# A four-layer graph attention stack: layer 2's all-node rows moved to blocks 3, 7 and 6, two projections per half step at its end, and ten of layer 3's units at the border

## The chip, the cores and the metric

The kernel runs on one core of a Trainium2 chip. The metric is the device time of one execution in microseconds (us), lower is better. A profile is one execution recorded by the hardware profiler; its engines are PE (matmuls), PEld (the weight loads beside them), DVE (vector), ACT (activation), POOL (GpSimd) and SP (which here only issues DMAs). SPq and POOLq are the queues on which SP and POOL issue DMAs.

## The reference, cut to what matters

4096 nodes with 256 features pass through four attention layers over one adjacency (1 in 256 entries set, and the diagonal). Layers 0 and 1 have four heads, layer 2 has two, layer 3 has one head with a positive and a negative softmax. Each layer ends in residual and layer norm, and the result is the input of the next.

```python
e = leaky_relu(s1[:, None, :] + s2[None, :, :], ALPHA)        # layer 2
e = where(adj[:, :, None] == 1, e, NEG)
h_prime = einsum('ijh,jhc->ihc', softmax(e, axis=1), W3h)
...
e = leaky_relu(Wh1 + Wh2.T, ALPHA)                            # layer 3
attention = softmax(where(mask, e, NEG_INF), axis=1)
negative_attention = -softmax(where(mask, -e, NEG_INF), axis=1)
new_h_prime = concatenate([attention @ x, negative_attention @ x], axis=1) @ fc_W
...
x = layernorm(x + layer(x))                                   # each of the four
```

## The kernel before, in words

The 4096 rows are 32 row tiles of 128 (`NT`), and eight blocks of four row tiles (`BT`, `NB`). A row tile attends in one of two ways.

A **packed** row tile uses 14 positions of 128 neighbours (`NP`): 13 gathers of neighbour rows from DRAM, issued by POOL as indirect DMAs (L636), and its own row tile, loaded by SP (L633). It works in two halves of seven positions (`RowTile.half`): ACT makes the weights position by position (L689 for layers 0 to 2; L666, L667 and L669 for layer 3), DVE masks them (L690; L668 and L670), PE multiplies them with the gathered rows (L701). The first six positions of every row hold only neighbours from row tiles 0 to 16 (`FRONT`, `MIX`, `NODES`), so a first half needs the projected rows 0 to 16 only, and a second half needs all 32.

A block in the **all-node** way takes four row tiles against all 32 node tiles with no gather (`Layer.whole_rows`). A unit of it is one node tile: a load of its rows (`vw`, L917) and, every eighth unit, of a mask (`mw`, L915), ACT and DVE for the weights (L929 and L930 in layer 2; L932, L934 or L936, and L937 in layer 3), four accumulations on PE (L940). `WHOLE = (0, 0, 3, 1)` puts the last three blocks of layer 2 (row tiles 20 to 31) and the last one of layer 3 (28 to 31) in this way; a block of layer 2 is 32 units, the one of layer 3 is 64 (32 for each softmax). Their mask is stored to DRAM while the neighbour lists are made, in layer 0 (L392, 2112 KB a block).

A layer goes in half steps: `Layer.part(m, part)` loads the packed tiles m and m+1, and `half_with_whole` projects one finished row of the next layer, runs the packed half, then as many units as spread the all-node work evenly over the steps up to three tiles before the end (`whole`). A projection (`Projection`) is a transpose of the row (L538), its copy to SBUF by ACT (L543), eight matmul records (L552), the row's values by ACT and DVE (L570 to L578), their store (L580), a transpose of the score row (L584) and its store (L591).

At the border, `Layer.close` projects the open rows below `MIX`, loads the first half of the following layer's tile 0, finishes the last tile, runs that first half, projects the rest, loads the first halves of tiles 1 and 2, runs tile 1's, and loads tile 3's. What the instruction streams of the engines look like is decided by the scheduler of the tile framework, which interleaves them within the limits of the data and of the buffers; each engine then runs its stream in that order.

Gathered rows lie in two pools, `g0` with 16 buffers and `g1` with 14. A layer 3 position fills a buffer; before, first halves lie in `g0` and second halves in `g1`. The PSUM banks of projections come from one pool of two (`ptwo[1]` in layer 2).

Of the kernel before, what the change touches and what calls it, by code (L numbers as in the profile page):

```python
# [53 lines left out]
NT = N // P  # L54
KT = F // P
BT = 4
W = BT * P
NB = NT // BT
# [14 lines left out]
CAP = NG * P  # L73
HALF = NP // 2

GROUPS = (((24, 4),), ((28, 2),), ((16, 2), (20, 1), (31, 2)), ((28, 1), (31, 4)))
LEAD = 10
MIX = 17
FRONT = 6
# [15 lines left out]

WHOLE = (0, 0, 3, 1)

LEAST = 2.0611536224385579e-09  # L100

# [76 lines left out]
class Turns:  # L178


    def __init__(self, pools):
        self.pools = list(pools)
# [6 lines left out]
class Program:  # L189
# [98 lines left out]
    def lists(self, ctx):  # L288
# [55 lines left out]
        for j in range(NT):  # L344
            m = 0
# [18 lines left out]
        class Block:  # L364
# [23 lines left out]

            def places(self):
                blk = self.blk  # L390
                if blk >= NB - max(WHOLE):
                    nc.sync.dma_start(out=shared["maskW"][blk], in_=self.mk)  # L392
                hit = wk.tile([P, BT, NT], BF16, name="hit")
                nc.vector.tensor_scalar(hit, self.red, 0.0, None, op0=ALU.is_gt)
                flat = hit.rearrange("p t j -> p (t j)")
                nc.vector.memset(flat[:, blk * BT:blk * BT + (BT - 1) * (NT + 1) + 1:NT + 1], 0.0)
                pt = prog.bank(prog.pthree)
                nc.tensor.matmul(pt[:, :P], flat, ones, start=True, stop=True)
                totals = wk.tile([P, P], BF16, name="totals")
# [59 lines left out]
        prog = self  # L459
# [140 lines left out]
class RowTile:  # L600

    def __init__(self, layer, m):
        self.layer, self.m = layer, m
        self.slots = {}
        self.accs = None

    def place(self, pos):


        L, n = self.layer, self.layer.n
        per = 1 if n == 3 else 2
        s = pos // per
        if s not in self.slots:
            pool = L.prog.g1 if n > 0 and s * per >= HALF else L.prog.g0
            self.slots[s] = pool.tile([P, 2 * ROW[0]], F32, name="G")
        c = (pos % per) * ROW[n]
        return self.slots[s][:, c:c + ROW[n]]
# [20 lines left out]
    def half(self, half):  # L640
# [1 line left out]
        prog, sh, S = L.prog, L.shared, self.S  # L642
        H, Wd, V, T, A = HEADS[n], WIDTH[n], VALS[n], TERMS[n], LOGS[n]
        if self.accs is None:
            pool = prog.ptwo[1 if n == 3 and self.m % 2 else 0]
# [78 lines left out]
class Layer:  # L724
# [2 lines left out]

    def __init__(self, prog, n):
        self.prog, self.n, self.nc, self.shared = prog, n, prog.nc, prog.shared
        self.count = NT - WHOLE[n] * BT  # L730
        self.tiles = {}
        self.loaded = set()
        self.units = self.whole_rows()
        self.total = WHOLE[n] * NT * (1 if n < 3 else 2)
        self.used = 0
        self.nxt = self.middle = self.stored = self.between = None
        self.group = []
        self.ready = []
        self.step = 0
        self.last = ()  # L740


    def tile(self, m):
        if m not in self.tiles:
            self.tiles[m] = RowTile(self, m)
        return self.tiles[m]

    def load(self, m, half):
# [4 lines left out]
    def set_banks(self):  # L753
        self.prog.banks = self.prog.ptwo[1] if self.n in (0, 2) else self.prog.pthree

    def whole(self, step):

        while self.between is None and self.used < self.total \
                and self.used < self.total * (step + 1) / (2 * self.count - 6):
            next(self.units)  # L760
            self.used += 1
        if self.used == self.total:
            next(self.units, None)

# [15 lines left out]
    def half_alone(self, m, part):  # L780


        self.step = 2 * m + part
        proj, middle = None, self.middle
        second = m > NT - (LEAD if self.n == 0 else 6) and len(self.ready) > 1
        if self.ready and self.ready[0][0] < self.step and (part == 0 or second):
            self.set_banks()
            if part == 1 and self.n == 0:
                self.prog.banks = self.prog.pthree
            proj = Projection(self.prog, self.n + 1, self.nxt, *self.ready.pop(0)[1:])  # L790
            proj.transpose()
        if part == 1 or self.tile(m).accs is None:
            self.tile(m).half(part)
        if self.stored is not None:
            self.stored.store()
# [12 lines left out]
        if middle is not None:  # L808
            middle.edge()
        self.stored, self.middle = middle, proj  # L810

    def half_with_whole(self, m, part):

        proj = None
# [12 lines left out]
        if self.between is not None:  # L827

            self.last = self.between()
            self.between = None  # L830
        if self.stored is not None:
            self.stored.store()
            self.stored = None
        if proj is not None:
# [5 lines left out]
        if proj is not None:  # L840
            proj.row()
            proj.edge()
            self.stored = proj

    def steps(self):
        for m in range(self.count):
# [3 lines left out]
    def close(self, following):  # L850

        last = self.count - 1
        self.step += 2
        if self.stored is not None:
            self.stored.store()
        if self.middle is not None:
            self.middle.row()
            self.middle.edge()
# [3 lines left out]
            self.set_banks()  # L862
            Projection(self.prog, self.n + 1, self.nxt, *entry[1:]).all()
        if following is not None:
            following.load(0, 0)
        if WHOLE[self.n]:
            for _ in self.units:
                pass
            self.tile(last).finish()
            if following is not None:  # L870
                following.tile(0).half(0)
        else:
            self.set_banks()
            first = Projection(self.prog, self.n + 1, self.nxt, *self.ready.pop(0)[1:])
# [617 lines left out]
```

## Time and profile before

| | us |
|---|---|
| median of 3 executions | 2267.64 (2262.25 to 2268.71) |
| the profiled execution | 2271.01 |
| its span, first to last instruction | 2269.3 |
| busy PE, DVE, ACT, POOL | 2019.7, 1798.0, 1738.5, 1494.7 |
| layer 2's first matmul of a packed half | 1340.7 |
| layer 3's first and last gather | 1746.65, 2240.07 |

The profiled execution lies 1.7 us over its span and 3.4 us over the median. Busy times are sums over all four layers and hide that each stage has another limit; so the prediction reads the stage around the change.

### The profile page before, as it was taken

What the parts mean: (1) busy time and instruction counts of PE and PEld (TensorE: products, weight loads), DVE (VectorE), ACT (ScalarE), POOL (GpSimd) and SP (SyncE); (2) the same over time, 40 slices, a digit from 0 to 9 for tenths busy, and PEclk for the clock granted to TensorE, in tenths of its full rate; (3) what the DMA queues carried; (4) which work ended last, traced back from release to release, by engine and by line L of the source; (5) the groups of instructions that cost most, each with busy time, mean ns of one, the idle gap of its engine ahead of it and who ended that gap; (6) DMA issues with size and microseconds to landing.
All of it is one profiled execution on the core that took longest, in us unless ns stands there. A gap on an engine that the chain in (4) does not pass through costs nothing. (4 is left out here: it accounts for less than half of the span.)

```text
span 2269.3 us, 49072 instructions
## 1 busy us (share of the span) xinstructions
PE 2019.7 (89%) x15689; PEld 1834.6 (81%) x15689; DVE 1798.0 (79%) x5317; ACT 1738.5 (77%) x4977; POOL 1494.7 (66%) x1596
## 2 busy tenths in 40 slices
PE   3878889989999959998988897989998799999996
PEld 2757878887989949998878887989997688778885
DVE  2987999999999959988888886877975465576567
ACT  4777888988889949988888877978883666676664
POOL 2107565655667777777777777777761677777773
PEclk8988999999999979999999998999998899999998
DMA  8879767877557766666666666778764788888884
GB/s 281 264 229 356 237 213 248 292 240 233 143 163 194 211 165 167 190 177 174 166 173 176 172 169 180 216 206 239 221 200 138 236 268 269 274 266 276 266 256 145
DMA packets 250318, 492.98 MB, mean 217 GB/s; under 512 B 44385, under 2 KB 156610, under 8 KB 249666
## 3 DMA queue, kind: packets, MB, share of 16 engines
q0 software_dynamic: 81536, 245.30, 38.0%
q1 hardware_dynamic: 168514, 244.46, 33.7%
q8 instruction: 126, 2.06, 0.4%
q14 instruction: 142, 1.16, 0.2%
HBM read 437.05 MB, written 52.54 MB: 216 GB/s over the span
## 5 line engine op out<-in xcount | busy, mean ns | idle before, releaser
L636 POOL DMA_INDIRECT G<-vals,idx x1456 | 1481.7, 1018 | 736.4 <-issue 188.5
L689 ACT ACTIVATE w<-S,G 128x128 f32<-128x128 f32 x3248 | 988.2, 389 | 123.0 <-DMA G<-vals,idx 109.1
L698 PE MATMUL bank<-w,G 128*65 128x128 f32 x7168 | 843.8, 277 | 97.8 <-DVE w L686 75.7
L698 PEld LDWEIGHTS bank<-w,G 128*65 128x65 f32 x7168 | 796.4, 140 | 116.5 <-DVE w L686 86.9
L701 PE MATMUL bank<-G,w 128*128 128x257 f32 (+1 forms) x2688 | 491.1, 340 | 36.1 <-DVE w L690 12.5
L701 PEld LDWEIGHTS bank<-G,w 128*128 128x128 f32 x2688 | 431.8, 193 | 86.2 <-ACT z L1004 16.6
L690 DVE SCALAR_TENSOR_TENSOR w<-w,bank 128x896 f32<-128x896 f32 x384 | 410.6, 1079 | 18.7 <-ACT w L689 18.1
L940 PE MATMUL bank<-vw,pw 128*128 128x129 f32 (+1 forms) x2048 | 299.7, 303 | 5.6 <-ACT zw L1004 2.7
L940 PEld LDWEIGHTS bank<-vw,pw 128*128 128x128 f32 x2048 | 275.7, 193 | 22.4 <-ACT zw L1004 3.1
L666 ACT ACTIVATE w<-S,G 128x128 f32<-128x128 f32 x392 | 138.0, 390 | 130.0 <-DMA G<-vals 77.6
L435 DVE TENSOR_SCALAR oh<-iota,place 128x256 bf16<-128x256 f16 (+2 forms) x992 | 225.8, 301 | 9.3 <-PE bank L441 9.3
L441 PE MATMUL bank<-mk,oh 128*128 128x132 fp8e4 x2336 | 188.6, 226 | 12.4 <-DVE oh L435 10.2
L680 DVE TENSOR_TENSOR w<-S,G 128x256 f32<-128x256 f32 x384 | 154.0, 417 | 53.0 <-DMA G<-vals,idx 49.6
L552 PE MATMUL bank<-wext,xT 128*128 128x268 f32 (+3 forms) x640 | 181.4, 417 | 15.7 <-ACT xT L543 12.8
L441 PEld LDWEIGHTS <-oh 128*128 128x128 bf16 x2336 | 148.6, 99 | 48.3 <-DVE oh L435 20.4
L380 ACT ACTIVATE mk<-raw 128x1024 uint8<-128x1024 int32 x128 | 131.1, 1054 | 25.8 <-DMA raw<-in_adjB_dram 25.1
L552 PEld LDWEIGHTS bank<-wext,xT 128*128 128x128 f32 x640 | 119.2, 203 | 35.5 <-ACT xT L543 15.7
L929 ACT ACTIVATE pw<-Sw,d 128x512 f32<-128x512 f32 x192 | 131.7, 714 | 15.6 <-PE bank L940 11.9
L937 DVE TENSOR_TENSOR pw<-pw,mw 128x512 f32<-128x512 f32 x64 | 44.1, 693 | 125.0 <-ACT pw L936 61.6
L930 DVE SCALAR_TENSOR_TENSOR pw<-pw,mw 128x512 f32<-128x512 f32 x192 | 126.7, 690 | 17.3 <-ACT pw L929 16.4
L686 DVE SCALAR_TENSOR_TENSOR w<-w,bank 128x896 f32<-128x896 f32 x128 | 138.6, 1083 | 0.8
L690 DVE SCALAR_TENSOR_TENSOR w<-w,mk 128x896 f32<-128x896 f32 x80 | 86.7, 1087 | 47.5 <-ACT w L689 44.1
(131 smaller groups left out, 1605.3 us busy)
## 6 DMA issues: line engine op xcount, KB each, us to landing
raw<-in_adjB_dram SPq DMA_DIRECT2D x128, 512.0 KB
mk<-maskC SPq DMA_DIRECT2D x112, 231.0 KB
G<-vals,idx POOLq DMA_INDIRECT x1456
S<-edge SPq DMA_DIRECT2D x64, 256.0 KB
vw<-vals SPq DMA_DIRECT2D x96, 129.0 KB
xp<-y SPq DMA_DIRECT2D x96, 128.0 KB
y<-xp SPq DMA_DIRECT2D x96, 128.0 KB
mw<-maskW SPq DMA_DIRECT2D x20, 528.0 KB
```

The source lines that it names most:

```text
L435: nc.vector.tensor_scalar(oh[:, :n * P], iota[:, :n * P], self.place[:, it, j:j + 1], None, op0=ALU.is_equal)
L441: nc.tensor.matmul(accs[b][:, s * MC:(s + 1) * MC], oh[:, (k - a) * P:(k - a + 1) * P], mk[:, j, it, :].bitcast(FP8), start=touches[b][0] ...
L552: nc.tensor.matmul(pp[:, :c1 - c0], self.xT[:, k, :], wext[:, k, c0:c1], start=(k == 0), stop=(k == KT - 1 and brow is None))
L636: nc.gpsimd.indirect_dma_start(out=self.place(pos), out_offset=None, in_=sh["v"][n][:NODES[t], :], in_offset=bass.IndirectOffsetOnAxis(ap= ...
L666: nc.scalar.activation(w[0][:, k, :], S[:, 0, :], AF.Relu, bias=d(k, 0))
L680: nc.vector.tensor_tensor(w[h][:, k:k + 2, :], S[:, h:h + 1, :].to_broadcast([P, 2, P]), dd[:, :, V + T + h:V + T + h + 1].to_broadcast([P ...
L686: nc.vector.scalar_tensor_tensor(w[h], w[h], LEAST, mh, op0=ALU.max, op1=ALU.mult)
L689: nc.scalar.activation(w[h][:, k, :], S[:, h, :], AF.Exp, bias=d(k, h))
L690: nc.vector.scalar_tensor_tensor(w[h], w[h], LEAST, mh, op0=ALU.max, op1=ALU.mult)
L698: nc.tensor.matmul(accs[0][:Wd, h * P:(h + 1) * P], v, w[h][:, k, :], **how)
L701: nc.tensor.matmul(a, w[h][:, k, :], v, **how)
L940: nc.tensor.matmul(accs[it][:, c:c + Wd], p[:, it, :], v[:, c:c + Wd], start=(j == 0 and h == heads[0]), stop=(j == NT - 1), skip_group_ch ...
```

## The change

Layer 2's all-node blocks are given by number and in order: 3, 7, 6 (row tiles 12 to 15, 28 to 31, 24 to 27). Its packed tiles are then 0 to 11 and 16 to 23, in this order, again 20. Layer 3 keeps block 7. Rows ready for projection are taken with those below `MIX` first. In layer 2's last three tiles, once its units are used up, a half step takes two projections, the second with banks of the pool `pthree`. At the border to layer 3 the first halves of four tiles are loaded together; tile 0's first half is followed by six units of layer 3, and each of the two rows still open by two more (`AHEAD` = 10), and the remaining units are spread over the layer as before. Layer 3's buffers: first halves of tiles 0 and 1 in `g0`, of 2 and 3 in `g1`, the second halves of these four in `g0`, and from tile 4 on, whole tiles in `g1` (even) and `g0` (odd). Rows of layer 2 are normed in other groups (`GROUPS`). The mask of block 3 instead of block 5 is stored to DRAM.

```diff
-GROUPS = (((24, 4),), ((28, 2),), ((16, 2), (20, 1), (31, 2)), ((28, 1), (31, 4)))
+GROUPS = (((24, 4),), ((28, 2),), ((16, 2), (17, 1), (20, 2), (24, 1), (31, 2)), ((28, 1), (31, 4)))
-WHOLE = (0, 0, 3, 1)
+WHOLE = ((), (), (3, 7, 6), (7,))
+AHEAD = 10
+ORDER = tuple([m for m in range(NT) if m // BT not in w] for w in WHOLE)
...
-                if blk >= NB - max(WHOLE):
+                if any(blk in w for w in WHOLE):
                     nc.sync.dma_start(out=shared["maskW"][blk], in_=self.mk)
...
-            pool = L.prog.g1 if n > 0 and s * per >= HALF else L.prog.g0
+            if n == 3:
+                other = self.step % 2 == 0 if self.step > 3 else self.step > 1 and s < HALF
+            else:
+                other = n > 0 and s * per >= HALF
+            pool = L.prog.g1 if other else L.prog.g0
...
-                and self.used < self.total * (step + 1) / (2 * self.count - 6):
+                and self.used < self.ahead + (self.total - self.ahead) * (step + 1) / (2 * self.count - 6):
...
     def half_with_whole(self, m, part):
-        if self.ready and self.ready[0][0] < self.step:
-            _, y, row = self.ready.pop(0)
-            self.set_banks()
-            proj = Projection(self.prog, self.n + 1, self.nxt, y, row)
-            proj.transpose()
+        able = sorted((e for e in self.ready if e[0] < self.step), key=lambda e: e[2] >= MIX)
+        self.set_banks()
+        over = self.used == self.total and m > self.count - 4
+        for entry, banks in zip(able, (self.prog.banks, self.prog.pthree)[:1 + over]):
+            self.ready.remove(entry)
+            projs.append(Projection(self.prog, self.n + 1, self.nxt, *entry[1:], banks=(banks,) * 3))
+            projs[-1].transpose()
...
     def close(self, following):
-            following.load(0, 0)
+            for m in range(4 if following.n == 3 else 1):
+                following.load(m, 0)
...
                 following.tile(0).half(0)
+                following.ahead = AHEAD
+                for _ in range(AHEAD - 2 * len(self.ready)):
+                    following.unit()
...
         for _, y, m in self.ready:
             self.set_banks()
             Projection(self.prog, self.n + 1, self.nxt, y, m).all()
+            if WHOLE[self.n]:
+                following.unit()
+                following.unit()
...
-        for blk in range(NB - WHOLE[n], NB):
+        for blk in WHOLE[n]:
```

More of the change, by code (lines that the diff above doesn't have):

```diff
@@ L600, with __init__ @@
 class RowTile:
-    def __init__(self, layer, m):
-        self.layer, self.m = layer, m
+    def __init__(self, layer, step, m):
+        self.layer, self.step, self.m = layer, step, m
         self.slots = {}
@@ L644, in half @@
         if self.accs is None:
-            pool = prog.ptwo[1 if n == 3 and self.m % 2 else 0]
+            pool = prog.ptwo[1 if n == 3 and self.step % 2 else 0]
             self.accs = [prog.bank(pool) for _ in range(2 if n == 3 else 1)]
@@ L729, in __init__ @@
         self.prog, self.n, self.nc, self.shared = prog, n, prog.nc, prog.shared
-        self.count = NT - WHOLE[n] * BT
+        self.order = ORDER[n]
+        self.count = len(self.order)
         self.tiles = {}
@@ L733, in __init__ @@
         self.units = self.whole_rows()
-        self.total = WHOLE[n] * NT * (1 if n < 3 else 2)
-        self.used = 0
-        self.nxt = self.middle = self.stored = self.between = None
+        self.total = len(WHOLE[n]) * NT * (1 if n < 3 else 2)
+        self.used = self.ahead = 0
+        self.nxt = self.middle = self.between = None
+        self.stored = []
         self.group = []
@@ L744, in tile @@
         if m not in self.tiles:
-            self.tiles[m] = RowTile(self, m)
+            self.tiles[m] = RowTile(self, m, self.order[m])
         return self.tiles[m]
@@ L754, in set_banks, with unit @@
         self.prog.banks = self.prog.ptwo[1] if self.n in (0, 2) else self.prog.pthree
+    def unit(self):
+        next(self.units)
+        self.used += 1
     def whole(self, step):
         while self.between is None and self.used < self.total \
-                and self.used < self.total * (step + 1) / (2 * self.count - 6):
-            next(self.units)
-            self.used += 1
+                and self.used < self.ahead + (self.total - self.ahead) * (step + 1) / (2 * self.count - 6):
+            self.unit()
         if self.used == self.total:
@@ L793, in half_alone @@
             self.tile(m).half(part)
-        if self.stored is not None:
-            self.stored.store()
+        for p in self.stored:
+            p.store()
         if proj is not None:
@@ L809, in half_alone @@
             middle.edge()
-        self.stored, self.middle = middle, proj
+        self.stored, self.middle = [middle] if middle is not None else [], proj
     def half_with_whole(self, m, part):
-        proj = None
+        projs = []
         self.step = 2 * m + part
-        if self.ready and self.ready[0][0] < self.step:
-            _, y, row = self.ready.pop(0)
-            self.set_banks()
-            proj = Projection(self.prog, self.n + 1, self.nxt, y, row)
-            proj.transpose()
+        able = sorted((e for e in self.ready if e[0] < self.step), key=lambda e: e[2] >= MIX)
[5 more added lines that the diff above has]
+            projs[-1].transpose()
         with ExitStack() as order:
@@ L830, in half_with_whole @@
             self.between = None
[L831 to L834, printed above, removed]
+        for proj in self.stored:
+            proj.store()
+        for proj in projs:
             proj.copy()
@@ L839, in half_with_whole @@
         self.whole(2 * m + part)
-        if proj is not None:
+        for proj in projs:
             proj.row()
             proj.edge()
-            self.stored = proj
+        self.stored = projs
     def steps(self):
@@ L853, in close @@
         self.step += 2
-        if self.stored is not None:
-            self.stored.store()
+        for proj in self.stored:
+            proj.store()
         if self.middle is not None:
```

## The prediction

> **What bounds the kernel now.** I read the stage around the change: layer 2's last half steps, the border, and layer 3, which runs to the end. First the costliest groups of the page, for POOL's gathers, and then the list of who waited for whom, for POOL alone in 1797 to 2245 us (us in total, times, longest).
>
> ```profile
> L636 POOL DMA_INDIRECT G<-vals,idx x1456 | 1481.7, 1018 | 736.4 <-issue 188.5
> ```
>
> ```profile
> POOL G L636 <- PE bank L701: 42.1, 134, 1.0
> POOL G L636 <- issue: 21.0, 69, 0.3
> POOL G L636 <- DMA G<-vals,idx: 15.8, 52, 0.3
> ```
>
> From 1797 on POOL waits in steps of 0.3 only, which stand before every gather whatever is named (134 x 0.3 is 40.2 of the 42.1). So POOL never stands still in layer 3: 331 gathers start between 1796.7 and 2240.1, 1.34 us each (mean 1.034 of issue and 0.30 between). PE waits for gathers instead. POOL's stream is the bound, and what counts is when it gets going. The same list for 1690 to 1797, and POOL's timeline:
>
> ```profile
> POOL G L636 <- ACT row L570: 54.8, 1, 54.8
> POOL G L636 <- issue: 13.6, 22, 7.2
> ```
>
> ```profile
> 1746.65 0.94 POOL L636 DMA_INDIRECT G<-vals,idx  x1 [54.82 <-ACT row L570]
> ...
> 1772.12 0.95 POOL L636 DMA_INDIRECT G<-vals,idx  x1 [0.30 <-issue]
> 1780.24 0.94 POOL L636 DMA_INDIRECT G<-vals,idx  x1 [7.17 <-issue]
> ...
> 1785.23 0.95 POOL L636 DMA_INDIRECT G<-vals,idx  x1 [0.30 <-issue]
> ```
>
> Two waits: 54.8 us for the store of row tile 16's values (the last below `MIX`), and 7.2 us, after 20 gathers, for that of row tile 19, without which no second half may be gathered. The 25th gather starts at 1785.23; from it to 2241.0 are 340 gathers in 455.8 us. Last, PE and ACT at the border by their timelines, and prices from the chain of waits:
>
> ```profile
> 1771.53 3.46 PE L552 MATMUL bank<-wext,xT 128*128 128x256 f32 x8 [3.00 <-ACT xT L543]
> ...
> 1800.08 9.27 PE L701 MATMUL bank<-G,w 128*128 128x257 f32 x28 [6.98 <-DVE w L668]
> ```
>
> ```profile
> 1750.55 0.40 ACT L666 ACTIVATE w<-S,G 128x128 f32<-128x128 f32 x1 [1.85 <-DMA G<-vals,idx]
> 1754.13 0.40 ACT L666 ACTIVATE w<-S,G 128x128 f32<-128x128 f32 x1 [3.18 <-DMA G<-vals,idx]
> 1754.44 0.15 ACT L570 ACTIVATE row<-bank 128x2 f32<-128x2 f32 x1
> ```
>
> ```profile
> 1707.43 3.13 PE bank L701 x28
> ...
> 1713.90 1.74 PE bank L552 x8
> ...
> 1830.53 6.07 PE bank L701 x28
> 1836.60 1.73 PE bank L940 x8
> ```
>
> A packed half costs PE 3.13 us in layer 2 and 6.07 in layer 3, a unit of layer 3 costs 1.73, a projection 1.74 and 0.33 for its transposes. A gather issued at 1746.65 is used at 1750.55, the next, of 1747.89, at 1754.13: 3.9 to 6.2 us. And an ACT operation that waits for a gather holds up a projection's row (L570) queued behind it.
>
> **What the Trainium skill says.** "GPSIMD Engine Reference", When to use GPSIMD: DMAs issued there have their descriptors made by GpSimd's own cores; the trace agrees, each gather keeps POOL 0.94 us or more. "Perfetto Trace Analysis", DMA Instruction — SWDGE (GPSIMD): the recorded end is that of descriptor generation, not of the data; agrees, 0.94 against the 3.9 to 6.2 above. "TensorE: Matmul & The Clock Gate", What's actually happening: an idle window of about 3.4 us halves PE's clock; agrees, after 6.98 idle the 28 records took 9.27 instead of 6.07. Same page, Architectural detail: ACT and DVE are strict FIFO; agrees with the L570 above.
>
> **The change, part by part.**
>
> *Which rows are late.* Rows 12 to 15 come from the first all-node block, so by my count of the steps all 17 rows below `MIX` are projected by half step 29 of 40 instead of after the last. The 54.8 us wait goes. The first 24 gathers (four first halves) are then late for their buffers only, which layer 2's tiles 20 to 23 free at half steps 32 to 39. By the changed kernel's instruction streams gather 25 is the first that waits for all 32 rows, the last being 23. So I work out when that row is stored.
>
> *PE up to it*, from 1707.2, the end of layer 2's last unit (step 33, equally many projections done in both: 22): six halves of layer 2, 6 x 3.13 = 18.8; eight projections (18; 19 and 24; 25 and 26; 27 and 20; 21), 8 x 2.07 = 16.6, three more than before; tile 0's first half 6.07: 1748.7. Then, by the stream, 34 of the 40 matmul instructions of the ten units (two records each, 1.73 / 8), 14.7, and projections 22 and 23, 4.1: 1767.5. From the end of the last projection's records to the gather took 5.25 before (1774.99 to 1780.24: row, store, landing): **1772.8**, 12.4 earlier than 1785.23. Second banks and the units as fill cost nothing extra: the units' work is in layer 3 anyhow, and eight of them have their weights made before, `dp` holding eight.
>
> *The wait that the change adds.* In ACT's new stream the 14 weights of tiles 0 and 1 stand among the rows of 19 to 27 and 21, and PE's stream puts each row's score transpose inside the next half. A gather into a buffer that a half has just freed is used, after 0.4 to 2.5 us of issue, 3.9 to 6.2 later; then come the row's exponential and DVE's row, 1.3; PE has 3.5 (two projections) and up to 1 more to bridge it. That stalls PE by 0 to 5 at each of four places (24; 26; 27 and 20; 21): 0 to 20 in all. DVE's masks of tile 1, and behind them row 21 and the norm of 23, wait with it; SP's loads of the own rows of tiles 2 and 1 wait likewise, with stores of rows behind them. I take 4.5, about 1 each, since a stall at one place also gives the next gather time: gather 25 at **1777.3**, 8 earlier.
>
> *After it.* POOL needs buffers of the halves before; PE, ahead by 13 us of units, frees them in time by its order (tile 1's first half is over before the second halves of tile 0 have landed). From 1748.7 PE has 55 halves x 6.07 + 64 units x 1.73 + 4.1 = 448.7, to 2197, while POOL from 1777.3 takes 455.8, to 2233; POOL stays the bound. The new buffer rule keeps the distance of two tiles; free. The tail from the last gather to the end, 28.3, stays. Units per half fall from 64/50 to 54/50; gathers exceed their least duration by 331 x (1.034 - 0.942) = 30, and if all of that came from the units a sixth would go, 4.7; 0 to 4.7, I take 1.
>
> *Layer 0.* The 2112 KB mask of block 5 went out at 378.1, where DVE was busy 56.68 of 57 us: no cost, so no gain in dropping it. That of block 3 falls near 200, into the stretch where DMA is full. Busy times by windows (PE, PEld, DVE, ACT, POOL, then clock, DMA share, GB/s):
>
> ```profile
> 215.00:225.00 10.00, 4.59 (x23) 4.20 (x24) 3.08 (x9) 6.14 (x19) 7.56 (x9) 0.52 1.02 382
> ...
> 245.00:255.00 10.00, 10.00 (x117) 9.65 (x116) 10.00 (x30) 10.00 (x27) 7.87 (x8) 1.00 0.62 170
> ```
>
> DVE starves there for adjacency loads, which SP now issues behind the mask: 2112 KB at 382 GB/s is 5.5. From 245 DVE is full and nothing gives it back. But ACT's new stream has fewer conversions ahead of the weights where it waited 5.9 us. From -2 to 5.5; I take 1. Layer 1 is unchanged, and block 3's rows, as early as block 5's were, feed the first units alike.
>
> Sum: -8 + 1 - 1 = -8, from the profiled 2271.0 to 2263.0, and from the median, 3.4 lower, **2259.6**.
>
> **The rivals.** *No stall at the border*: POOL 12.4 earlier, -12.4 in all, 2255.2. For it: PE was full in layer 2's last steps before. Against: the FIFO waits above. *Slower*: in-order waits on gathers become the bound of the border, 5 at each of the four places, 20 instead of 4.5: gather 25 at 1792.8, +7.6, 2275.2. For it: 24 gathers now share DMA with layer 2's own loads, and the 3.18 wait with L570 behind it. Against: 5 is the worst landing everywhere. It decides from gather 25 later than 1785.2. *Nothing*: stalls of about 8 leave 4, layer 0's full 5.5 eats it: about 2268. For it: the starving DVE at 215. *PE as the bound of layer 3*: the end would be near 2197 and the tail, a gain of over 40; excluded by POOL's 455.8.
>
> **How the numbers follow.** A measurement tells about 0.3%, 6.8 us, from no change. Likeliest case 0.45, own range 2256 to 2265, three quarters of it faster than 2260.8; no stall 0.19; nothing 0.18; slower 0.18. Faster 0.54, same 0.27, slower 0.19. Low end: no stall, with 4.7 from the gathers instead of 1, and 2 gained in layer 0 for 1 lost, 2248.5; high end: the slower rival.
>
> **What would show it.** Right: the first gather of layer 3 before 1715; 24 by about 1760; then one wait of 15 to 20 for the row store, ending near 1777; 1.34 per gather after; a last gather near 2232. Wrong: PE's idle time before L587 (score transposes) beyond 10 in 1715 to 1755; waits of POOL on PE over 0.3 in layer 3; layer 2's first packed half over 3 us later than 1340.7.

## The result, and the profile after

| | before | after |
|---|---|---|
| median, measured together | 2267.64 (5 runs) | 2278.46 (5 runs, 2276.01 to 2283.02) |
| the profiled execution, its span | 2271.01, 2269.3 | 2283.02, 2280.9 |
| layer 3's first gather, its 24th, its 25th | 1746.7, 1784.0, 1785.2 | 1695.1, 1756.7, 1793.1 |
| last gather, from there to the end of the span | 2240.1, 29.2 | 2244.8, 36.1 |

The changed kernel is slower: ratio 1.0056, 95% interval 1.0036 to 1.0076. A second comparison of the same two kernels gave 1.0055 (1.0036 to 1.0074). The forecast was 2259.6.

First POOL between 1690 and 1850: who it waited for (us in total, times, longest), and its timeline (start, duration, wait before it).

```profile
POOL G L644 <- DMA vw<-vals: 35.5, 1, 35.5
POOL G L644 <- PE bank L709: 27.3, 20, 8.5
POOL G L644 <- ACT erow L593: 8.3, 2, 4.8
```

```profile
1756.68 0.94 POOL L644 DMA_INDIRECT G<-vals,idx  x1 [0.30 <-ACT w L674]
1793.09 0.94 POOL L644 DMA_INDIRECT G<-vals,idx  x1 [35.46 <-DMA vw<-vals]
```

The 54.8 us wait of before is gone and 24 gathers are done by 1757.6, as forecast. But then POOL stands 35.5 us, not 15 to 20, and gather 25 starts 7.9 later than before. (The releaser named, a load of `vw`, is not what the gather needs; it needs row 23 stored, as the first experiment shows.) What stands ahead of row 23, by PE's timeline:

```profile
1731.77 3.65 PE L555 MATMUL bank<-wext,xT 128*128 128x256 f32 x16
1738.38 0.27 PE L587 MATMUL bank<-ident,row 128*1 128x128 f32 x1 [2.97 <-DVE row L581]
...
1761.23 6.36 PE L709 MATMUL bank<-G,w 128*128 128x257 f32 x22
1767.43 10.56 PE L964 MATMUL bank<-vw,pw 128*128 128x257 f32 x48
...
1784.85 2.01 PE L555 MATMUL bank<-wext,xT 128*128 128x256 f32 x8
```

The 2.97 is one of the stalls before a score transpose. At 1767.43 tile 0's first half is over and six of the ten units run in one piece; the last projection ends only at 1786.86. ACT's timeline shows where the 2.97 comes from:

```profile
1732.42 0.39 ACT L674 ACTIVATE w<-S,G 128x128 f32<-128x128 f32 x1
1737.11 0.40 ACT L674 ACTIVATE w<-S,G 128x128 f32<-128x128 f32 x1 [4.30 <-DMA G<-vals,idx]
1737.42 0.15 ACT L573 ACTIVATE row<-bank 128x2 f32<-128x2 f32 x1
```

A weight of layer 3 waits 4.30 for its gather, and the 0.15 us exponential of a row, queued behind it, waits too. In PE's list of waits of 1705 to 1770 the score transposes cost 7.7 (5.4, 1.9 and 0.4).

Last, PE in layer 3 (its waits for `z`, 1797 to 2290), before and after:

```profile
PE bank L701 <- ACT z L1004: 12.2, 10, 2.4
```

```profile
PE bank L709 <- ACT z L1028: 23.1, 11, 7.7
```

PE waits twice as long for `z`, the copy that frees its accumulators; with its waits for weights it stands 33.7 in all, 26.3 before. The last and longest wait for `z` stands 43 us before the end. By the timelines of PE, SP, ACT and DVE:

```profile
2237.76 26.78 PE L709 MATMUL bank<-G,w 128*128 128x257 f32 x112 [7.69 <-ACT z L1028]
```

```profile
2225.18 0.34 SPq L1016 DMA_DIRECT2D out_dram<-y  x1
2225.69 0.86 SPq L641 DMA_DIRECT2D G<-vals  x2
```

```profile
2233.24 0.69 ACT L674 ACTIVATE w<-S,G 128x128 f32<-128x128 f32 x2 [9.77 <-DMA G<-vals]
...
2237.23 0.47 ACT L1028 ACTIVATE z<-bank,recp 128x256 f32<-128x256 f32 x1 [0.94 <-DVE recp L1025]
```

```profile
2234.95 1.09 DVE L676 TENSOR_TENSOR w<-w,mk 128x896 f32<-128x896 f32 x1 [9.80 <-ACT w L675]
...
2237.03 0.16 DVE L1025 RECIPROCAL recp<-bank 128x1 f32<-128x1 f32 x1
```

`G<-vals` without an index is not a gather: it is the own row tile of a packed tile, loaded by SP, here behind the store of a finished output tile. A weight on ACT waits 9.77 for it, DVE's masks wait 9.80 for ACT, the reciprocal that `z` needs stands behind these masks, and PE, which was through with its last half at 2230.07 (2237.76 less 7.69), waits for `z`.

From 2237.76 PE runs four halves without a pause, while POOL's last gather is issued at 2244.84: the end is PE's, and comes 36.1 after that gather instead of 29.2.

### The profile page after: what moved, and what is told of

Same layout as the page of the kernel before. It is cut to its first block, busy times and chain, and to the rows that moved or that the text cites. A ratio compares the mean times of both kernels' runs of the same rounds, so it can differ in the third digit from the quotient of the medians.

```text
span 2280.9 us, 49073 instructions
## 1 busy us (share of the span) xinstructions
PE 2026.3 (89%) x15689; PEld 1841.1 (81%) x15689; DVE 1797.4 (79%) x5317; ACT 1739.3 (76%) x4977; POOL 1494.8 (66%) x1596
## 5 line engine op out<-in xcount | busy, mean ns | idle before, releaser
L697 ACT ACTIVATE w<-S,G 128x128 f32<-128x128 f32 x3248 | 988.3, 389 | 123.7 <-DMA G<-vals,idx 111.0
L709 PE MATMUL bank<-G,w 128*128 128x257 f32 (+1 forms) x2688 | 505.4, 347 | 44.5 <-ACT z L1028 23.1
L709 PEld LDWEIGHTS bank<-G,w 128*128 128x128 f32 x2688 | 444.0, 199 | 96.1 <-ACT z L1028 28.2
L698 DVE SCALAR_TENSOR_TENSOR w<-w,bank 128x896 f32<-128x896 f32 x384 | 410.5, 1079 | 22.4 <-ACT w L697 21.4
L674 ACT ACTIVATE w<-S,G 128x128 f32<-128x128 f32 x392 | 138.6, 391 | 150.4 <-DMA G<-vals 80.1
L688 DVE TENSOR_TENSOR w<-S,G 128x256 f32<-128x256 f32 x384 | 153.7, 415 | 54.4 <-DMA G<-vals,idx 44.2
L555 PE MATMUL bank<-wext,xT 128*128 128x268 f32 (+3 forms) x640 | 175.2, 406 | 10.8 <-ACT xT L546 8.0
L698 DVE SCALAR_TENSOR_TENSOR w<-w,mk 128x896 f32<-128x896 f32 x80 | 86.7, 1088 | 49.0 <-ACT w L697 48.9
L676 DVE TENSOR_TENSOR w<-w,mk 128x896 f32<-128x896 f32 x56 | 61.0, 1090 | 77.1 <-ACT w L675 75.5
```

The costliest lines, as they stand in the source:

```text
L555: nc.tensor.matmul(pp[:, :c1 - c0], self.xT[:, k, :], wext[:, k, c0:c1], start=(k == 0), stop=(k == KT - 1 and brow is None))
L674: nc.scalar.activation(w[0][:, k, :], S[:, 0, :], AF.Relu, bias=d(k, 0))
L688: nc.vector.tensor_tensor(w[h][:, k:k + 2, :], S[:, h:h + 1, :].to_broadcast([P, 2, P]), dd[:, :, V + T + h:V + T + h + 1].to_broadcast([P ...
L697: nc.scalar.activation(w[h][:, k, :], S[:, h, :], AF.Exp, bias=d(k, h))
L698: nc.vector.scalar_tensor_tensor(w[h], w[h], LEAST, mh, op0=ALU.max, op1=ALU.mult)
L709: nc.tensor.matmul(a, w[h][:, k, :], v, **how)
```

## The experiments

My theory after this: the loss is in three places that don't depend on each other, the units ahead of the last projections, the in-order waits of ACT, and something in layer 3 that makes PE late. The rivals: PE as the bound of layer 3, so that nothing at the border matters; the added mask store in layer 0; and the choice of blocks itself. The stages that separate them, from each run's own profile: "border" is from the end of layer 2's last unit to gather 25, "layer 3" from gather 25 to the end of the span. Times are medians; the fifth column is their distance to the median of the kernel before measured beside them, and gains are read from that column, except between two runs that were measured together.

| run | border | layer 3 | median | to before | ratio to before, 95% |
|---|---|---|---|---|---|
| before | 77.8 | 484.1 | | 0 | |
| after | 79.9 | 487.8 | 2278.46 | +10.8 | 1.0056 (1.0036-1.0076) |
| after_again | 81.2 | 490.2 | 2280.53 | +13.2 | 1.0055 (1.0036-1.0074) |
| projs_first | 66.0 | 493.1 | 2269.44 | -0.1 | 0.9992 (0.9982-1.0003) |
| rows_first | 71.3 | 490.1 | 2271.20 | +1.7 | 1.0004 (0.9996-1.0011) |
| oldrule | 78.2 | 482.4 | 2272.38 | +5.0 | 1.0024 (1.0013-1.0036) |
| both | 57.1 | 489.8 | 2261.24 | -8.1 | 0.9962 (0.9951-0.9974) |
| both_spread | 57.7 | 492.8 | 2259.69 | -9.6 | 0.9960 (0.9944-0.9976) |
| both_late | 57.0 | 491.7 | 2258.84 | -10.5 | 0.9958 (0.9942-0.9973) |
| both_old | 57.5 | 483.4 | 2252.90 | -16.4 | 0.9935 (0.9917-0.9953) |
| both_old_2 | 57.3 | 484.4 | 2253.34 | -13.9 | 0.9946 (0.9927-0.9965) |
| best | 57.7 | 485.0 | 2251.94 | -15.4 | 0.9927 (0.9902-0.9951) |
| both_old_one | 62.4 | 485.0 | 2259.24 | -8.1 | 0.9959 (0.9947-0.9970) |
| three_old_blocks_2 | 61.5 | 486.0 | 2254.23 | -13.0 | 0.9940 (0.9923-0.9958) |
| old_blocks | 78.4 | 492.3 | 2277.30 | +7.8 | 1.0029 (1.0019-1.0040) |
| mask3 | 76.7 | 487.3 | 2273.55 | +4.0 | 1.0024 (1.0015-1.0033) |
| mask3_2 | 75.9 | 491.5 | 2271.14 | +3.9 | 1.0016 (1.0006-1.0026) |
| mask3_late_2 | 76.2 | 486.0 | 2269.52 | +2.3 | 1.0012 (1.0003-1.0020) |

Where the border begins varies between profiled executions from 1704.2 to 1714.6, the same kernel by 6 (after 1713.2, after_again 1706.8). So absolute times of single profiles compare badly. The border compares well: in before and the three kernels that only store a mask more it is 75.9 to 77.8. Layer 3 compares less well, 484.1 to 491.5 in these four (the profile of mask3_2, 7.0 over its own median, has the 491.5).

**projs_first.** In `close`, the last two projections go ahead of the units:

```diff
-                for _ in range(AHEAD - 2 * len(self.ready)):
-                    following.unit()
...
         for _, y, m in self.ready:
             self.set_banks()
             Projection(self.prog, self.n + 1, self.nxt, y, m).all()
-            if WHOLE[self.n]:
-                following.unit()
-                following.unit()
+        if WHOLE[self.n] and following is not None:
+            for _ in range(AHEAD):
+                following.unit()
```

> The changed kernel, except that the last two projections (rows 22 and 23) come ahead of the ten units of layer 3 at the border instead of after six of them and between the rest. Theory 'row 23 is late behind the units': the changed kernel's gather 25 waits 35.5 us for row 23's store, and 10 x 1.73 = 17.3 us of units stand ahead of that store; gather 25 then starts near 1767.4 (end of tile 0's first half) + 2 x 2.07 + about 1 of gaps + 6.4 (store to gather) = 1779, 14 earlier than 1793.1, and the time falls by 10 to 14, to 2264-2268. Rival 'PE is the bound of layer 3 by now': PE's work after 1767 is the same, so an earlier POOL start is given back as waits of POOL for buffers; gather 25 moves by 14 as well, but POOL then waits on PE by more than 0.3 per gather and the time falls by less than 5, to 2274-2278. Rival 'stalls elsewhere': gather 25 moves by less than 5.

Measured: border 66.0, 14 to 15 less than after; time 11 to 13 us less. POOL's timeline and PE's:

```profile
1773.83 0.95 POOL L644 DMA_INDIRECT G<-vals,idx  x1 [20.54 <-DMA vals<-row]
```

```profile
1766.82 1.90 PE L555 MATMUL bank<-wext,xT 128*128 128x256 f32 x8
...
1769.97 13.17 PE L964 MATMUL bank<-vw,pw 128*128 128x257 f32 x60
```

Only the order of projections and units changed, gather 25 follows the last projection, and the releaser named is now a store of values. So gather 25 does wait for row 23, and the units ahead of it cost POOL what they last. PE took little of the gain back: 11 to 13 of the 14 to 15 arrived, where the rival of PE as the bound expected under 5.

**rows_first.** ACT's weights of layer 3's tiles 0 and 1 are ordered behind the latest projected row (for layer 3 only):

```diff
-        nc.scalar.activation(vals[:, :, D:], ...
+        self.prog.latest = nc.scalar.activation(vals[:, :, D:], ...
...
-                following.tile(0).half(0)
+                with self.prog.behind(following.n):
+                    following.tile(0).half(0)
...
-            following.tile(1).half(0)
+            with self.prog.behind(following.n):
+                following.tile(1).half(0)
...
+    def behind(self, n):
+        return self.tc.issue_after(self.latest.ins) if n == 3 else ExitStack()
```

> The changed kernel, except that ACT's weights of layer 3's tiles 0 and 1 (first halves) are ordered behind the exponential of row 21, so that none of them stands ahead of a projection's row in ACT's queue; no gather moves. Theory 'in-order waits of ACT on gathers hold up the rows': PE's idle time before the score transposes (L587) in 1713 to 1767 falls from 8.2 to under 3, tile 0's first half ends near 1762 for 1767.4, gather 25 starts 5 to 8 earlier than 1793.1, and the time falls by 4 to 8, to 2270-2274. Rival 'the waits only change place' (tile 0's weights come later and PE waits for them instead): gather 25 moves by less than 2 and the time stays at 2276-2281.

Measured: border 71.3, 8.6 to 9.9 less; time 9 to 11 less. PE's waits of 1705 to 1770, the complete list for the score transposes:

```profile
PE bank L587 <- DVE u L1011: 1.9, 1, 1.9
PE bank L587 <- DVE row L575: 0.6, 1, 0.6
```

7.7 became 2.5, the waits did not change place, and the theory of the in-order queue stands. POOL's gathers keep their order. PE's order changes a little too, above all by three of the ten units, which the scheduler put ahead of tile 0's first half, so the run shows what both together are worth. PE also ran faster: from the last unit to the end of that half it was busy for 42.4 (47.6 less 24 records of units at 1.73 / 8) at a granted clock of 1.00, and for 46.2 at 0.94 in the changed kernel.

**mask3, mask3_2, mask3_late, mask3_late_2.** The kernel before with block 3's mask stored too, at the changed kernel's place or two packed tiles later:

```diff
-                if blk >= NB - max(WHOLE):
+                if blk >= NB - max(WHOLE) or blk == 3:
                     nc.sync.dma_start(out=shared["maskW"][blk], in_=self.mk)
```

```diff
             def pack(self, it):
                 m, mk = self.blk * BT + it, self.mk
+                if self.blk == 3 and it == 2:
+                    nc.sync.dma_start(out=shared["maskW"][3], in_=mk)
```

> The kernel before, plus one thing: block 3's mask (2112 KB) is also stored in layer 0, as the changed kernel does; nothing reads it. Theory 'the store delays the gather stream for good': gathers start about 3.2 us later than in the kernel before from layer 0's end on (the first of layer 2 near 1325 for 1322.0), because POOL never stops in layers 1 and 2, and the time rises by 3 to 6, to 2271-2274. Rival 'the store is hidden': gathers within 1 us of before, time within 1.5 of before's, 2266-2269.

> The kernel before with block 3's mask stored too, once more beside the late store: 3 to 5 over the kernel before, as the first time (ratio 1.0024), if that was no accident.

> The kernel before with block 3's mask stored as well, but two packed tiles later than in the run that added it (which came 4 us over the kernel before). Theory 'it is the place, where DMA is full, that costs': within 1.5 of before, 2266-2270. Rival 'it is the 2112 KB wherever they go, or another order of layer 0': 3 to 5 over before, 2270-2274.

> The kernel before with block 3's mask stored two packed tiles later, once more: within 1.5 of before by the theory that the place costs, 3 to 5 over it by the rival that the bytes cost wherever they go.

Measured: +4.0 and +3.9 with the store, +2.3 with the late one. The price of the first theory, but not its mechanism: the first gather of layer 2 came at 1320.9 and 1321.1, where before had 1322.0, so no delay is seen in the gather stream. The 2.3 fits neither expectation (within 1.5, or 3 to 5), and the intervals of the early store and of the late one overlap, so whether place or bytes cost stays open too. mask3_late ran on a chip where every kernel was slower (see the end): 2.2 over a before of 2769.01 (1.0010, 0.9994 to 1.0025), which decides nothing.

**old_blocks.** The changed kernel with the blocks and groups of before:

```diff
-GROUPS = (..., ((16, 2), (17, 1), (20, 2), (24, 1), (31, 2)), ...)
-WHOLE = ((), (), (3, 7, 6), (7,))
+GROUPS = (..., ((16, 2), (20, 1), (31, 2)), ...)
+WHOLE = ((), (), (5, 6, 7), (7,))
```

> The changed kernel with the all-node blocks of before (5, 6, 7, so rows 20 to 31) and its groups; two projections per half step, the ten units, the early loads and the new buffer rule stay. Theory 'the choice of blocks costs (mask of block 3, gathers of layers 1 and 2 late) and the border costs': gathers of layers 1 and 2 as in before (first of layer 2 near 1322), layer 2's first unit near 1352 for 1358; the first gather of layer 3 after 1720 since row 16 is late again, gather 25 near 1787 (six less than 1793.1), time 2270-2275. Rival 'the early rows matter most': without them the 24 gathers crowd in front of gather 25, which starts later than 1795, time over 2280.

Measured: +7.8, that is 3 to 5 below the changed kernel. The first gather of layer 3 comes at 1732.6, 37 us after the changed kernel's, and the border is no longer for it. Both theories missed something: the early gathers are not what decides, and layer 3 was late here as well (492.3), with a long stretch after the last gather. In the profiles of after, projs_first, rows_first and this one it was 34.3 to 38.5, in those of before and mask3 29.2 and 30.1.

**both.** The edits of projs_first and rows_first together.

> The changed kernel with both edits: the last two projections ahead of the ten units, and ACT's weights of layer 3's tiles 0 and 1 behind the exponential of row 21. Alone they gave 9 and 7 us. Theory 'two separate costs in one chain up to gather 25': gather 25 near 1765 (19.3 earlier through the order of the units in projs_first, up to 12.3 in rows_first, so some 24 to 30 together against 1793.1, less what the two share), time 2260-2265. Rival 'PE is the bound once POOL starts before 1775': gather 25 as early, but the end stays with PE: last gather near 2228, the rest after it over 38, time 2266-2270.

Measured: border 57.1, -8.1 to before. The border is 23 to 24 below the changed kernel's, where the two edits alone gave 14 to 15 and 9 to 10: they add up, and the time is the first theory's (gather 25 came at 1771.7 for 1765, in a profile whose border began late, at 1714.6). PE's waits (1797 to 2290) still have the long ones:

```profile
PE bank L709 <- ACT z L1028: 18.9, 8, 4.9
```

**both_old, both_old_2.** As both, with the old rule for buffers from the fifth tile on:

```diff
-                other = self.step % 2 == 0 if self.step > 3 else self.step > 1 and s < HALF
+                other = s >= HALF if self.step > 3 else self.step > 1 and s < HALF
```

> The kernel with both edits, and the old buffer rule for layer 3 from the fifth tile on (first halves in one pool, second halves in the other). Theory 'the new buffer rule makes the end late': the stretch from the last gather to the end was 29 to 30 us in the two kernels with the old rule and 34 to 38 in the four with the new one; with the old rule here it is 29 to 31 again, and the time 4 to 6 below that of the kernel with both edits. Rival 'it is the ten units (all of layer 3 has another phase), not the rule': the stretch stays at 34 or more, and the time within 2 of the kernel with both edits.

> The kernel with three edits once more, beside the one above on the same chip: 2250-2255 where the kernel before takes 2267-2270 (ratio 0.9935 before).

Measured: 2252.90, 8.3 below both, and 2253.34, 5.8 below it by the distance to before; layer 3 483.4 and 484.4 for 489.8; the stretch after the last gather 29.6 and 29.3 for 33.0. PE's and POOL's instructions stand in the same order in both kernels. Those of ACT, DVE and SP don't. On ACT, between an exponential (L677) and the `z` that follows it stands one weight (L674) of a later half under the old rule, and one and two in turn under the new, through most of layer 3. The two timelines of ACT at such a place, the new rule (both) and the old (both_old):

```profile
1918.09 0.39 ACT L674 ACTIVATE w<-S,G 128x128 f32<-128x128 f32 x1
1919.00 0.40 ACT L674 ACTIVATE w<-S,G 128x128 f32<-128x128 f32 x1 [0.53 <-DMA G<-vals,idx]
1919.46 0.47 ACT L1028 ACTIVATE z<-bank,recp 128x256 f32<-128x256 f32 x1
```

```profile
1907.40 0.40 ACT L674 ACTIVATE w<-S,G 128x128 f32<-128x128 f32 x1
1908.71 0.47 ACT L1028 ACTIVATE z<-bank,recp 128x256 f32<-128x256 f32 x1 [0.90 <-DVE recp L1025]
1909.08 0.76 ACT L674 ACTIVATE w<-S,G 128x128 f32<-128x128 f32 x2
```

In the first, `z` comes out behind a gather's landing, and PE's next half starts at 1919.99 after 1.62 of idle "<-ACT z". In the second `z` waits only for its own reciprocal. So the 16 and 14 buffers, dealt out by tile, gave no later wait for a buffer (POOL 0.3 at most from 1850 on, SP's loads of own rows 0.4 at most), but another order on ACT, DVE and SP.

The stall that counts most runs through all three queues, as in the changed kernel above. In each of the eight profiles with the new rule ACT waits 6.8 to 9.8 for an own row some 48 us before the end, and PE then stands 4.9 to 7.7 for `z`; SP had issued the last two own rows 16 to 20 us before the last gather. In the ten with the old rule, that of before among them, they were issued 21 to 28 us before it, and PE's longest wait for `z` in the last 50 us is 3.7. Which of the three orders is to blame was not separated by a run.

**oldrule.** The same line alone, in the changed kernel.

> The changed kernel with the old buffer rule for layer 3 from the fifth tile on; PE's and POOL's order are the same as the changed kernel's, only ACT's, DVE's and SP's differ. Theory 'under the new rule ACT's weights of the next half stand ahead of z (L1028), which frees PE's accumulators, and one of them waits for a gather or the own row': PE's idle time before L709 that ends with z falls from 23.1 in 1797-2290 to 11-13, the stretch from gather 25 to the end falls from 487.8 to 480-484, time 4 to 8 below the changed kernel's. Rival 'the rule costs only when POOL starts early': less than 3 below.

Measured: 8.2 below after_again, measured beside it; layer 3 482.4, waits for `z`, and the longest of the last 50 us:

```profile
PE bank L709 <- ACT z L1028: 11.2, 10, 3.0
```

```profile
2225.26 8.02 PE L709 MATMUL bank<-G,w 128*128 128x257 f32 x28 [2.48 <-ACT z L1028]
```

In all PE stands 30.7 for 33.7: most of what it no longer waits for `z` it now waits for weights (14.8 for 6.2). So the sum of its waits doesn't tell the gain. The stall that went is the one near the end: at 2237.76, in the changed kernel, POOL has only 7 us to its last gather, and from PE's start to the end of the span it is 43.

**after_again.** The changed kernel as it is.

> The changed kernel once more, on the chip of this call, as the reference for the single edits: by every theory 2276-2281 at a time of before of 2267-2270.

**both_spread.** As both, with `AHEAD = 0`.

> The kernel with both edits, without the ten units at the border: all 64 units of layer 3 are spread over its half steps as in the kernel before. Theory 'the ten units fill a wait and cost nothing': PE then stands idle after tile 0's first half until the first second half has its gathers, some 10 to 17 us, POOL's gather 25 is unmoved, and the time rises by 0 to 5 as PE gets to the end later. Rival 'the ten units make the end late': the stretch after the last gather falls from about 35 to 29-31, and the time falls by 4 to 6.

Measured: 1.6 below both, no more than the runs scatter; PE stands idle for weights for 5.9 just after the border, less than the 10 to 17 expected. The stretch after the last gather is 34.5, so the rival's 29 to 31 did not come. The ten units behind the projections neither help nor harm; they are not what makes the end late.

**both_late** and **best.** As both and as both_old, each with the mask of block 3 stored in `pack` as in mask3_late and left out in `places`.

> The kernel with both edits, and block 3's mask stored two packed tiles later in layer 0 (some 25 us, where DVE is full and DMA is not). Theory 'the store costs because it falls where DMA is full' (one added store cost 4 us of the median in the kernel before): time 3 to 5 below the kernel with both edits, gathers from the 104th on 2 to 4 earlier. Rival 'it costs wherever it is, or the scheduling of layer 0 is what costs': within 1.5.

> The changed kernel with all four edits: the last two projections ahead of the units, ACT's weights of tiles 0 and 1 behind row 21, the old buffer rule, block 3's mask stored later. Theory 'four separate costs': 2249-2252 (2252.9 with three of them, and 1 to 4 for the mask). Rival 'POOL and PE are both close to full in layer 3, so the mask's gain is lost': 2252-2255.

Measured: both_late 2.4 below both; best 15.4 below before, where both_old had 16.4 and 13.9. Neither stands out of the scatter of the runs. **best** is faster than before and than the changed kernel: 0.9927 (0.9902 to 0.9951) to before, as is both_old (0.9935).

**both_old_one.** As both_old, with one projection per half step:

```diff
-        over = self.used == self.total and m > self.count - 4
+        over = False
```

> The kernel with three edits (projections ahead of the units, weights behind row 21, old buffer rule), with one projection per half step at layer 2's end instead of two. Theory 'two per half step bring the last rows out of the border': four or five projections more stand between the halves' end and row 23, each 2.07, and with the gaps between them gather 25 is 5 to 12 later than 1765.7, time 4 to 10 over the kernel with three edits. Rival 'PE's work up to row 23 is the same sum whatever the order': gather 25 within 2, time within 2.

Measured: border 62.4 for 57.4; 8.1 below before, where both_old had 16.4 and 13.9. The second projection per half step is worth 6 to 8.

**three_old_blocks, three_old_blocks_2.** As both_old, with blocks 5, 6, 7 and the groups of before.

> The kernel with three edits (projections ahead of the units, weights behind row 21, old buffer rule), with the all-node blocks of before (5, 6, 7) and its groups. Theory 'the moved rows are worth little, since what decides is row 23 or 19, the last packed row': the first gather of layer 3 comes near 1730 instead of 1691, but 24 of them are still done before the last row is stored, near 1765; gather 25 within 3 of 1765.7, no mask of block 3 is stored (4 us in the kernel before), and the time is 2248-2253, equal to or below that of the kernel with three edits. Rival 'the early rows are what the gain rests on': gather 25 after 1772 and the time 2258 or more.

> The kernel with three edits and the blocks of before (5, 6, 7), once more, since on the chip of the last call the kernel before itself took 2769 us. Theory 'the moved rows are worth little once the three costs are gone': within 3 of the kernel with three edits beside it. Rival 'the early rows are what the gain rests on': 5 to 10 over it, with gather 25 more than 5 later.

Measured, second time: 2254.23 beside 2253.34. Border 61.5 for 57.3: the 24th gather starts at 1763.3, and gather 25 follows at 1766.6 after a wait of 2.4, for 18.9 with the new blocks, so here POOL's own 24 gathers are nearly the limit. The moved rows thus make the border 4 us shorter, but the kernel with old blocks stores no mask of block 3, which costs about as much (mask3). In all they bring no measurable gain. The first time the chip was another, see the end.

## Why the prediction was wrong

Two of its terms failed. The stalls at the border, taken at 4.5 us, came to 12.9: 8.2 of waiting, and 4.7 of slower work that went with it. And the buffer rule, taken as free, cost about 8. The mask, taken at 1, cost about 4. Step by step:

*The 54.8 us wait goes, 24 gathers by about 1760, then one wait that ends with row 23's store; POOL then runs through.* Right in kind (1695.1, 1757.6, waits of 0.3 from 1850 on); the one wait lasted 35.5, not 15 to 20. The 54.8 us themselves were worth nothing measurable, and the prediction did not price them: gather 25 needs the last row, and by the order in the code the last packed row is projected at the same half step with either choice of blocks. With blocks 5, 6 and 7 the border of the changed kernel is 78.4, with the new ones 79.9 and 81.2.

*PE up to row 23.* The prediction's span from the last unit to gather 25 was 70.1 (1777.3 less 1707.2); measured 79.9 and 81.2. Term by term in the profiled execution:
- six halves, eight projections and tile 0's first half: 41.5 and 4.5 of stalls, 46.0, were forecast. It took 54.4. PE was idle for 8.2 of it, and its 46.2 of busy time are 4.7 over the price. This is the mis-sized term: 4.5, "about 1 each", for 8.2 and 4.7. The slower work went with the stalls: the granted clock was 1.00 from 1726 to 1735, 0.57 from 1740 to 1744, after the wait of 2.97, 0.59 from 1760 to 1764, around that of 2.44, and 0.94 over the whole; in rows_first, with most of the stalls gone, it stayed at 1.00 and the busy time was 0.9 over the price. So the clock fell with waits of 2.97 and 2.44, shorter ones than the window of about 3.4 us that the prediction cites, and the prediction counted no slower work. The slower rival had 20 for the term, with 5 at each of four places; the longest single wait was 2.97. The rival's gather 25 (1792.8 for 1793.1) came true, but by luck: about half of the 15.8 came from other terms.
- units and the two last projections: 18.8 forecast, 19.3 measured. The sum had the ten units in the chain to gather 25 and priced them well. What failed is the sentence on them, "the units as fill cost nothing": their work is in layer 3 anyhow, but put ahead of row 23 they cost POOL 14 to 15 us of border (projs_first), while both_spread shows that behind it they cost nothing.
- store to gather: 5.25 forecast, 6.2 measured.
- The rest of the distance, 1793.1 for 1777.3, is where the border began: 1713.2 for 1707.2. The repeat began it at 1706.8, so that is no part of the change.

*The in-order wait that the change adds.* Right as a mechanism and named at the right queue: "ACT/DVE are strict FIFO" (the Trainium skill, "TensorE: Matmul & The Clock Gate", Architectural detail) agrees with the 4.30 above. Taking it away gave 9 to 11 us, twice the 4.5 that I took.

*"The new buffer rule keeps the distance of two tiles; free."* Wrong, and the largest error after the border: 8.2 by oldrule, 8.3 and 5.8 by both_old. I looked for a later release of a buffer, and there is none: POOL never waits over 0.3 from 1850 on. What the rule changed is the order on ACT, DVE and SP, and with it the last own rows came later, held up ACT and DVE and made PE late for the end. That the scheduler reordered them because the rule changes its own estimate of when a buffer is free is my reading; no run shows its reasons. My test "waits of POOL on PE over 0.3 in layer 3" looked at the wrong engine; "the tail ... stays", 28.3 from the end of the last gather, is what fell (34.8; 36.1 from that gather's start).

*Units per half, 1 gained.* POOL took 452.9 from gather 25 on, 2.9 less than the 455.8 of before and within the 0 to 4.7 given. But this stretch was 456.8 to 462.3 in the kernels that only store a mask more, so one profile doesn't show a gain, and PE ended the layer anyhow.

*Layer 0, 1 lost.* About 4 by mask3 and mask3_2. Within the bounds of -2 to 5.5, but the working behind them (adjacency loads late behind the store) isn't confirmed: the test I gave, layer 2's first packed half, stood at 1340.7 in the profile of the changed kernel too (at 1336.2 in after_again). No border of the mask's runs shows the 4; their layer 3 is 1.9 to 7.4 above the one profile of before, which can as well be scatter.

*PE as the bound of layer 3* was excluded by POOL's 455.8, and this was too simple. POOL's share holds. But PE was close enough behind it that one stall of 7.7 before its last four halves moved the end.

Together: the border 10 over its forecast, layer 3 some 5 to 7 over 483, the mask 3 over its 1; that is the distance from 2259.6 to 2278.5.

## What to carry to other kernels

- Find the last row that a stage waits for before you make the others early; here 42 us of earlier gathers (1691.5 for 1733.5) made the border 4 us shorter and were worth nothing measurable with the mask that they need, while the order of the last two projections and the units was worth 11 to 13.
- Put fill work behind the work that releases the bound engine (14 to 15 us of the border here), and anything that waits for a slow transfer behind the small operations that others wait for in the same in-order queue (9 to 10 us here).
- A stall of the matmul engine can cost twice: 8.2 us of waits at the border went with 4.7 us of slower work after them.
- A change of buffers can cost without a longer wait for a buffer, if the scheduler answers it with another order: compare the order of every engine's instructions and of the DMA issues, and look at the stalls near the end, where there is no slack to hide them.

## What I had not expected of the hardware

- One chip ran the kernel before in 2769.01 (43 runs) and three_old_blocks in 2776.52 (ratio 1.0027, 1.0011 to 1.0043), 22% longer than the 2267 to 2270 on the other chips here. Single operations last as long as elsewhere (L697 on ACT 389 ns on both chips, L698 on DVE 1081 and 1077); but PE pauses in the middle of a run of matmuls for no wait that the profile shows, and the granted clock is 0.889 for 0.960. From PE's timeline there:

```profile
1407.52 0.38 PE L706 MATMUL bank<-w,G 128*65 128x128 f32 x2 [1.04 <-issue]
1408.97 0.30 PE L706 MATMUL bank<-w,G 128*65 128x128 f32 x1 [1.07 <-issue]
1410.36 2.29 PE L706 MATMUL bank<-w,G 128*65 128x128 f32 x10 [1.10 <-issue]
```

  There the gain of the three edits (with the old blocks) is gone. The cause was not looked for and is open.
- POOL's gather stream differs by some 5 us between executions of one kernel from layer 0 on: the changed kernel's first gather of layer 2 came at 1325.3 and, the second time, at 1320.7.
